# Four lanes of 24 to 28 quads instead of three of 32, with the later sorts' copies on GpSimd

## The chip, the cores and the metric

The kernel runs on one core of a Trainium2 chip. The metric is the device time of one execution in microseconds (us); lower is better. In the profile PE is TensorE's matmul, PEld its weight load, DVE VectorE, ACT ScalarE, POOL GpSimd and SP the engine that issues most of the DMAs.

## The reference

One layer of a graph network over V = 100,000 nodes of 64 channels and E = 3,300,000 edges, which come sorted by their target:

```python
h = jnp.maximum(_layernorm(x, axis=-1), 0.0)
local, nbr = h[dst], h[src]
y = jnp.concatenate([local, nbr - local], axis=-1) @ W.T + b      # per edge
s, cnt = segment_sum(y, dst, V), segment_sum(1, dst, V)
out = x + where(cnt > 0, s / max(cnt, 1), 0)
```

The sum over a node's edges is linear, so the kernel needs, per node, the sum of its neighbours' h, the count of its edges, and the node's own h times a weight matrix (the "own part").

## The kernel before

**First stage** (lines 207 to 315): per step of 3,584 nodes it loads `xt`, makes h by layer norm and relu, splits h into three bf16 parts and writes them as rows of `h3`, so that a sum of the three is as good as fp32. It clears the accumulator `acc` in DRAM, and it makes the own part (transpose on PE, copy `hT` on ACT, two matmuls, copy `own` on ACT) and writes that to `hb`.

**Two ways for the edges.** 384 windows of 8,064 consecutive edges go through a sort; what is left over, 57 chunks of 3,584 edges, is gathered. For a chunk (`chunks`, line 365) GpSimd issues 28 indirect DMAs of 128 rows of `h3` each (`nb`, line 403), DVE makes one-hot matrices `hot`, and PE sums the rows per target into `ps`.

**Lanes.** A lane is a set of windows, one per partition. `sort_lane` (line 430) loads a window's targets and sources, packs both into a key, and sorts the 8,192 keys of each partition by source with a merge network. `exchange` (line 468) is one step of it on a piece of at most 1,536 (lane 0) or 1,024 keys: a copy of the lower halves to `tmp` on ACT (line 469), then a min and a max on DVE (lines 470 and 471). Lane 0 has its `tmp` in PSUM, the later ones in SBUF. `fill_lane` (line 635) then fetches the sorted keys of each of the 157 source blocks of 640 nodes by indirect DMA (`kf`, line 650; `kx`, line 735) and writes tables of slots for the next stage (`sr_d`, `dt_d`).

**Quads.** `quads` (line 761) takes four windows at a time. For every source block it needs a one-hot `gh` (DVE, line 809) that picks rows of the block's table `tab` by matmul into `gp` (line 832), a cast of `gp` to `gs` on ACT (line 834), a second one-hot `dh` (DVE, line 360), and matmuls of both into `total` (line 841). Four blocks are a group: one `gh`, one `dh`, up to 24 matmuls of line 832 and 64 of line 841. `gh` has two buffers, `gp` two in lane 0 and three later. Tables of three blocks each are streamed from DRAM for each quad (727.5 KB a load), but every `STAY`th one is kept in SBUF (`stay`): none in lane 0, every 6th in lane 1, every 3rd in lane 2. A quad has 2,592 matmuls of line 841, so their count says how many quads a stretch holds.

**What runs beside what.** The sort of lane 0 runs with the chunks' gathers; `fill_lane(0)` follows. Then the quads of lane l run with the sort and the fill of lane l+1 between them: after each pick of a block (a `yield` of `quads`) `SORT` is taken from `spent`, and sort steps are issued until their estimates (`2.083 * n + 290` for n keys, close to ns) have filled it again. Lane 0's quads also carry the chunks that are left; the last lane runs alone, in a loop of two turns. After that come corrections for windows that share a node, and a last stage (line 1049) that divides, multiplies by the other weight matrix and writes `out`. The framework orders each engine's instructions by a schedule of its own, so a sort step can stand earlier than its place in the code.

Of the kernel before, what the change touches and what calls it, by code (L numbers as in the profile page):

```python
# [32 lines left out]
LANES = 3  # L33
# [5 lines left out]
STEP = 1000  # L39
SORT = 260  # L40
STAY = None, 6, 3
# [20 lines left out]
PIECES = 1536, 1024, 1024  # L62
# [23 lines left out]
def plan(v, e):  # L86

    wl = 1 << int(np.log2(33 * CH * 1.05))
    ew = wl - PAD
    nw = LANES * P  # L90
    return wl, nw, -(-(e - nw * ew) // CHUNK)
# [3 lines left out]
def gnn_preln(ctx: ExitStack, tc, x, src_w, dst_w, src_p, dst_p, src_a, dst_a, wT, b, out, V, E):  # L95
# [27 lines left out]
    SETS = NL * G  # L123
# [11 lines left out]
    assert 2 * C == P and SL % GP == 0 and NCB % GP and G % TURNS == 0  # L135
# [50 lines left out]

    x_v = x.rearrange("(p t) c -> p t c", p=P)
# [19 lines left out]
    with tc.tile_pool(name="pre", bufs=2) as pre, tc.tile_pool(name="small", bufs=4) as small, \  # L207
# [19 lines left out]
        b_sb = pre.tile([P, C], F32, name="b_sb", bufs=1)  # L227
        nc.sync.dma_start(b_sb, b.to_broadcast([P, C]))
        b3 = pre.tile([3 * 32, 2, C], BF16, name="b3", bufs=1)
        nc.vector.memset(b3, 0.0)  # L230
        b_part = pre.tile([P, C], BF16, name="b_part", bufs=1)
        for i in range(3):
            nc.vector.tensor_copy(b_part, b_sb)
            nc.vector.tensor_sub(b_sb, b_sb, b_part)
            nc.vector.tensor_copy(b3[32 * i:32 * i + 1], b_part[32 * i:32 * i + 1, None, :].to_broadcast([1, 2, C]))
        ones3 = pre.tile([3 * 32, P], BF16, name="ones3", bufs=1)
        nc.vector.memset(ones3, 1.0)


# [34 lines left out]
        for t in range(0, NPT, T):  # L274
            load_x(t + 2 * T)
            nc.sync.dma_start(acc_v[:, t:t + T], zeros)
            xt = xts.pop(t)
            st = st_ps.tile([P, 5, T], F32, name="st")
            nc.vector.tensor_reduce(st[:, 0], xt, axis=AX.X, op=ALU.add)
            nc.vector.tensor_scalar_mul(st[:, 1], st[:, 0], 1.0 / C)  # L280
            nc.vector.tensor_sub(xt, xt, st[:, 1, :, None].to_broadcast([P, T, C]))
            sq = pre.tile([P, T, C], F32, name="sq", bufs=3)
            nc.scalar.activation(sq, xt, AF.Square)
            nc.vector.tensor_reduce(st[:, 2], sq, axis=AX.X, op=ALU.add)
            nc.scalar.activation(st[:, 3], st[:, 2], AF.Sqrt, bias=eps, scale=1.0 / C)
            nc.vector.reciprocal(st[:, 4], st[:, 3])
            nc.vector.scalar_tensor_tensor(xt, xt, 0.0, st[:, 4, :, None].to_broadcast([P, T, C]), op0=ALU.max, op1=ALU.mult)

            parts = pre.tile([P, T, CT], BF16, name="parts", bufs=3)
            nc.gpsimd.memset(parts[:, :, C3:], 1.0)  # L290
            nc.scalar.copy(parts[:, :, :C], xt)
            nc.gpsimd.tensor_tensor(sq, xt, parts[:, :, :C], ALU.subtract)
            nc.scalar.copy(parts[:, :, C:2 * C], sq)
            nc.gpsimd.tensor_tensor(parts[:, :, 2 * C:C3], sq, parts[:, :, C:2 * C], ALU.subtract)
            nc.sync.dma_start(h3_v[:, t:t + T], parts)
            own = pre.tile([P, T, C], F32, name="own")
            for u in range(0, T, SUB):
                n = min(SUB, T - u)
                t_ps = st_ps.tile([P, SUB // 2, P], F32, name="t_ps")
                for i in range(n // 2):  # L300
                    nc.tensor.transpose(t_ps[:, i], xt[:, u + 2 * i:u + 2 * i + 2].rearrange("p a c -> p (a c)"), ident)
                hT = pre.tile([P, SUB // 2, P], F32, name="hT")
                nc.scalar.copy(hT[:, :n // 2], t_ps[:, :n // 2])  # L303
                o_ps = st_ps.tile([P, SUB, C], F32, name="o_ps")
                o2 = o_ps.rearrange("p (i a) c -> p i (a c)", a=2)
                for i in range(n // 2):
                    nc.tensor.matmul(o2[:, i], lhsT=ones3, rhs=b3.rearrange("p a c -> p (a c)"), start=True, stop=False)
                    nc.tensor.matmul(o2[:, i], lhsT=hT[:, i], rhs=w_own.rearrange("p a c -> p (a c)"),  # L308
                                     start=False, stop=True)
                nc.scalar.copy(own[:, u:u + n], o_ps[:, :n])  # L310
# [6 lines left out]
    with tc.tile_pool(name="few", bufs=1) as few, ExitStack() as early:  # L317
# [17 lines left out]
        def store(base, at, tiles):  # L335

            with after(SP):
                row = nc.values_load(base, engines=[SP], min_val=0, max_val=V)
                for i, part in enumerate(tiles):
                    if i:  # L340
                        nc.sync.dma_start(acc[ds(row + i * P, P)], part)
                    else:
                        last[SP] = nc.sync.dma_start(shared[at], part[0:1])
                        nc.sync.dma_start(acc[ds(row + 1, P - 1)], part[1:])

        later = []
# [5 lines left out]
        def add_now(all_of_them=False):  # L352
            while later and (all_of_them or (later[0][0] <= count[0] and count[0] - count[1] >= GAP)):
                later.pop(0)[1]()
                count[1] = count[0]
# [9 lines left out]
        def chunks(n):  # L365
# [22 lines left out]
            for k in range(n * parts + 1):  # L388
                q, part = divmod(k, parts)
                u = q % KG  # L390
                if q < n:
                    if u == 0 and part == 0:
                        si, near = ahead
                    hot = rows.tile([P, JH, P], BF16, name="hot", bufs=4)
# [21 lines left out]
                if before is not None and before[2] == parts - 1:  # L416
                    sums = rows.tile([P, C1], F32, name="sums", bufs=LAG + 2)
# [9 lines left out]
        def drain(events):  # L427
            for _ in events:
                pass
        def sort_lane(l, keys, piece, few, ps):  # L430
# [13 lines left out]
            mine = slice(l * P, l * P + P)  # L444
            for x in range(2):
                for i in range(W):
                    nc.sync.dma_start(wb_d[x, mine].rearrange("(g i) o -> i g o", i=W)[i], wb_i[i * G:i * G + G, x:x + 1])
                nc.sync.dma_start(wb_r[:, x, mine], wb_d[x, mine].rearrange("w o -> o w"))
# [19 lines left out]
            def exchange(lo, hi, tmp):  # L468
                last[ACT] = nc.scalar.copy(tmp, lo)  # L469
                nc.vector.tensor_tensor(lo, tmp, hi, ALU.min)  # L470
                last[DVE] = nc.vector.tensor_tensor(hi, tmp, hi, ALU.max)  # L471

            def merge(p, k):
# [3 lines left out]
                def blocks(b, q, m):  # L477
                    r = keys[:, 2 * p * b:2 * p * (b + q)].rearrange("p (b l) -> p b l", l=2 * p)
                    if k < p:
# [4 lines left out]
                             tmp[:, :q * m * k].rearrange("p (b m t) -> p b m t", b=q, t=k))  # L484

                def run(a, n):
                    tmp = ps.tile([P, PIECE], F32, name="tmp")
                    exchange(keys[:, a:a + n], keys[:, a + k:a + k + n], tmp[:, :n])

                def groups(a, n):  # L490
                    r = keys[:, a:a + 2 * k * n].rearrange("p (m s t) -> p m s t", s=2, t=k)
                    tmp = ps.tile([P, PIECE], F32, name="tmp")
                    exchange(r[:, :, 0], r[:, :, 1], tmp[:, :n * k].rearrange("p (m t) -> p m t", t=k))
# [72 lines left out]
            for t in range(len(tail) + 2 * regions):  # L566
                for i in range(regions):
                    q = t - 2 * i
                    if 0 <= q < len(tail):
# [8 lines left out]
                        if q == len(tail) - 1:  # L578
                            ready = min(span * (i + 1), WL)
# [5 lines left out]
            assert ready == WL  # L585
# [49 lines left out]
        def fill_lane(l, piece, took):  # L635
# [3 lines left out]
            mine = slice(l * G, l * G + G)  # L639
# [16 lines left out]
            def spread(numbers, n, to):  # L656
# [90 lines left out]
            nc.sync.dma_start(xs_d[:, mine], xg)  # L747
# [161 lines left out]

        def behind_quads(l, aside):  # L910
# [9 lines left out]
        with tc.tile_pool(name="keys", bufs=1) as big, tc.tile_pool(name="piece", bufs=2) as piece, \  # L920
                tc.tile_pool(name="sort_ps", bufs=2, space=PSUM) as ps:
            for i, ns in enumerate(sort_lane(0, big.tile([P, WL], F32, name="keys"), piece, few, ps)):
                k = i - 40
                if 0 <= k < NCB:
                    with tc.issue_after(last[ACT].ins):
                        nc.scalar.dma_start(tables[k // TG, :, k % TG].rearrange("p (b f) -> p b f", b=NB),
                                            h3[k * CS:(k + 1) * CS].rearrange("(b p) f -> p b f", b=NB))
                gathers(ns)

        for l in range(NL):  # L930
            with ExitStack() as aside:
# [7 lines left out]
                else:  # L939
                    early.close()  # L940
                with tc.tile_pool(name="load", bufs=3) as load, tc.tile_pool(name="hots", bufs=3) as hots, \
                        tc.tile_pool(name="g_ps", bufs=3 if l else 2, space=PSUM) as g_ps, \
# [3 lines left out]
                    if l == NL - 1:  # L946
                        with tc.For_i(0, TURNS, 1) as g:
                            drain(quads(l * G + g * (G // TURNS), G // TURNS, kept))
# [11 lines left out]
                    if l == 0:  # L960
                        drain(ev)
# [163 lines left out]
```

## Time and profile before

| What | us |
|---|---|
| median of 3 runs (lowest, highest) | 22121.42 (22117.3, 22134.35) |
| the profiled execution, whole | 22127.49 |
| its span, first to last instruction | 22125.9 |
| mean granted TensorE clock | 0.869 of full |

The profiled execution is 6.1 us above the median. Its span falls into stages, and the engines' busy shares over the whole span mix them, so the reading goes by stage: where each stage begins and ends is seen by which lines run in it. The first stage ends near 460 us, the sort of lane 0 near 1650, the first fill at 2013, lane 0's quads at 10000, lane 1's at 16560, lane 2's at 21770.

### The profile page before, as it was taken

To read this page: it belongs to the slowest core of one execution; us is meant where nothing else is said; L and a number is where in the kernel's file an instruction comes from. 1 tells how busy PE (TensorE), PEld (TensorE's weight loads), DVE (VectorE), ACT (ScalarE), POOL (GpSimd) and SP (SyncE) were. 2 spreads that over 40 slices of the span, in tenths; PEclk is the share of its full clock that TensorE was granted. 3 is DMA by queue.
4 is the path that set the end of the run, shared out by engine and by line. 5 is a ranking of instruction groups with operands and counts; after the bars stand their busy time and mean duration, and the time that the engine had idled before them with its cause. 6 is when DMAs were issued, how large, how long until landed. Compare 5 with 4: busy or idle time off the path is not lost. (4 is left out here: it accounts for less than half of the span.)

```text
span 22125.9 us, 770402 instructions
## 1 busy us (share of the span) xinstructions
PE 16188.9 (73%) x343607; PEld 13895.5 (63%) x343607; DVE 15051.3 (68%) x13757; ACT 8886.6 (40%) x17494; POOL 2886.3 (13%) x2647
## 2 busy tenths in 40 slices
PE   5102556567777688887777777776888999899996
PEld 4002444456665577776666666665777888788886
DVE  8894444457665566667777777765767777777775
ACT  4342222234443344443444444533444444444442
POOL 5763333310002100000000000011000000000003
PEclk7556777788888899999999999987999999999998
DMA  6544545566666677786666666666777777677777
GB/s 247 80 68 114 160 150 159 154 194 223 214 226 217 212 266 267 268 268 225 217 219 214 217 218 212 218 209 181 260 257 239 241 235 238 227 231 241 236 239 261
DMA packets 1821829, 4713.39 MB, mean 213 GB/s; under 512 B 951238, under 2 KB 959697, under 8 KB 1813057
## 3 DMA queue, kind: packets, MB, share of 16 engines
q1 hardware_dynamic: 1629646, 4493.73, 61.7%
q0 software_dynamic: 80656, 105.27, 3.0%
q10 hardware_dynamic: 108188, 64.99, 1.4%
q8 instruction: 2692, 44.11, 0.8%
q14 instruction: 647, 5.30, 0.1%
HBM read 4466.78 MB, written 235.40 MB: 213 GB/s over the span
## 5 line engine op out<-in xcount | busy, mean ns | idle before, releaser
L832 PEld LDWEIGHTS <-gh 128*128 128x128 bf16 x90432 | 7799.2, 101 | 4935.9 <-issue 3557.5
L834 ACT CAST gs<-gp 128x386 bf16<-128x386 f32 x15072 | 7131.9, 482 | 9211.9 <-PE gp L832 8091.3
L832 PE MATMUL gp<-tab,gh 128*128 128x193 bf16 x75264 | 7998.1, 258 | 3657.2 <-ACT gs L834 1727.4
L809 DVE TENSOR_TENSOR gh<-srs,c 128x3072 bf16<-128x3072 int16 (+1 forms) x3840 | 6617.0, 1723 | 4745.8 <-PE gp L832 4452.1
L841 PE MATMUL total<-gs,dh 32*128 32x193 bf16 x241152 | 6720.4, 255 | 591.8 <-issue 567.0
L841 PEld LDWEIGHTS <-dh 32*128 32x128 bf16 x241152 | 5408.2, 98 | 1656.2 <-issue 1612.1
L360 DVE TENSOR_TENSOR dh<-dt,c 128x2048 bf16<-128x2048 int16 (+1 forms) x3840 | 4586.7, 1194 | 1499.2 <-PE total L841 775.2
L469 ACT COPY tmp<-keys 128x1024 f32<-128x1024 f32 (+16 forms) x948 | 1017.0, 1081 | 2727.5 <-DVE keys L471 2380.5
L798 POOL DMA_INDIRECT rows_x<-h,xs x192 | 181.9, 947 | 14093.4 <-PE total L841 10876.8
L403 POOL DMA_INDIRECT nb<-h,si x1596 | 1633.0, 1023 | 2097.8 <-PE ps L408 1573.2
L832 PE MATMUL gp<-stay,gh 128*128 128x193 bf16 x15168 | 1536.4, 250 | 161.3 <-ACT gs L834 147.9
L471 DVE TENSOR_TENSOR keys<-tmp,keys 128x1024 f32<-128x1024 f32 (+16 forms) x948 | 1173.6, 1252 | 19.8
L470 DVE TENSOR_TENSOR keys<-tmp,keys 128x1024 f32<-128x1024 f32 (+14 forms) x948 | 1160.7, 1239 | 17.1 <-ACT tmp L469 16.3
L408 PE MATMUL ps<-nb,hot 128*128 128x193 bf16 x1596 | 357.9, 307 | 1059.8 <-DVE sums L421 673.6
L408 PEld LDWEIGHTS <-hot 128*128 128x128 bf16 x1596 | 190.0, 122 | 1098.1 <-DVE sums L421 682.1
L650 POOL DMA_INDIRECT kf<-ksort,at_i x483 | 459.9, 952 | 1073.3 <-ACT k L691 908.9
L860 DVE SCALAR_TENSOR_TENSOR whole<-own,whole 128x193 f32<-128x193 bf16 x768 | 285.7, 414 | 123.4 <-ACT whole L856 123.3
L856 ACT COPY whole<-total 128x388 f32<-128x388 f32 x384 | 157.4, 497 | 237.9 <-PE total L841 218.1
L864 DVE TENSOR_REDUCE wsums<-whole 128x128 f32<-128x384 f32 x384 | 226.9, 591 | 0.1
L308 PEld LDWEIGHTS o_ps<-w_own,hT 128*128 128x128 f32 x784 | 160.7, 260 | 94.9 <-ACT hT L303 84.3
L735 POOL DMA_INDIRECT kx<-ksort,xat x192 | 181.1, 943 | 298.0 <-DVE xat L732 240.4
L308 PE MATMUL o_ps<-w_own,hT 128*128 128x128 f32 x784 | 193.5, 386 | 14.8 <-ACT hT L303 14.2
(189 smaller groups left out, 3677.7 us busy)
## 6 DMA issues: line engine op xcount, KB each, us to landing
tab<-tables SPq DMA_DIRECT2D x4160, 727.5 KB
srs<-sr_d SPq DMA_DIRECT2D x1824, 512.0 KB
tables<-h ACTq DMA_DIRECT2D x157, 242.5 KB
h<-parts SPq DMA_DIRECT2D x28, 1358.0 KB
own<-h SPq DMA_DIRECT2D x384, 97.0 KB
srs<-sr_d SPq DMA_DIRECT2D x96, 320.0 KB
dt_d<-t SPq DMA_DIRECT2D x57, 512.0 KB
dt<-dt_d SPq DMA_DIRECT2D x1824, 16.0 KB
```

What stands on the lines that cost most here:

```text
L308: nc.tensor.matmul(o2[:, i], lhsT=hT[:, i], rhs=w_own.rearrange("p a c -> p (a c)"), start=False, stop=True)
L360: nc.vector.tensor_tensor(out.rearrange("p k (a d) -> p k a d", d=D), numbers[:, :, None].to_broadcast(shape), upto[:shape[0], :n].rearran ...
L403: last[POOL] = nc.gpsimd.indirect_dma_start(out=nb[:, j], out_offset=None, in_=h3, in_offset=bass.IndirectOffsetOnAxis(ap=si[:, u, at:at + ...
L408: nc.tensor.matmul(ps, lhsT=before[0][:, j], rhs=before[1][:, j, :CE], start=before[2] == 0 and j == 0, stop=before[2] == parts - 1 and j ...
L469: last[ACT] = nc.scalar.copy(tmp, lo)
L470: nc.vector.tensor_tensor(lo, tmp, hi, ALU.min)
L471: last[DVE] = nc.vector.tensor_tensor(hi, tmp, hi, ALU.max)
L650: last[POOL] = nc.gpsimd.indirect_dma_start(out=kf[:, c], out_offset=None, in_=ksort, in_offset=bass.IndirectOffsetOnAxis(ap=at_i[:, c0 + ...
L809: last["hots"] = nc.vector.tensor_tensor(gh[:, :m].rearrange("p c i b s -> p (c i) b s"), srs[u, s // SL][:, c:c + m].rearrange("p c i s - ...
L832: nc.tensor.matmul(gp[:, i], lhsT=ghots[u, s][:, i, b], rhs=row[:, b + i * (NB - NR), :CE], start=b == 0, stop=b == NR - 1)
L834: nc.scalar.copy(gs[u, s], gp)
L841: nc.tensor.matmul(total[:, i, to(b)], lhsT=hot[at, b * P:b * P + P], rhs=of[at], start=flags.get("start", False) and b == 0, stop=flags.g ...
```

## The change

The number of lanes goes from three of 32 quads to four of 24, 24, 24 and 28, so 400 windows are sorted instead of 384, and 21 chunks are gathered instead of 57. All chunks are issued before the first quads (`drain(ev)` stands ahead of them), so lane 0's quads no longer share PSUM and SBUF with them: they get three `gp` buffers and every 6th table kept; `STAY` is 6, 6, 6, 3. Each lane still sorts 128 partitions; those without a window of their own repeat another. The fill writes only the rows of the lane's own quads. `SORT` goes from 260 to 340. Lane 0's pieces shrink from 1,536 to 1,024 keys. In lanes 1 to 3 the copy to `tmp` moves from ACT to GpSimd and is issued one piece ahead: the min and max of the piece before follow it (`held`). The own part leaves the first stage: that writes h itself to `hb`, and `own_part` reads it back, makes the product and writes it again, one step per sort step of lane 0 from the tenth on; the clearing of `acc` goes there too, on ACT's queue instead of SP's.

```diff
+QUADS = 24, 24, 24, 28
+LANES = len(QUADS)
-STEP = 1000
-SORT = 260
-STAY = None, 6, 3
+SORT = 340
+STAY = 6, 6, 6, 3
-PIECES = 1536, 1024, 1024
+PIECES = 1024, 1024, 1024, 1024
+HEAD = 10
...
         for t in range(0, NPT, T):
-            nc.sync.dma_start(acc_v[:, t:t + T], zeros)
...
-            own = pre.tile([P, T, C], F32, name="own")
-            for u in range(0, T, SUB):
...
-            nc.scalar.dma_start(hb_v[:, t:t + T], own)
+            nc.scalar.dma_start(hb_v[:, t:t + T], xt)
...
-            def exchange(lo, hi, tmp):
-                last[ACT] = nc.scalar.copy(tmp, lo)
-                nc.vector.tensor_tensor(lo, tmp, hi, ALU.min)
-                last[DVE] = nc.vector.tensor_tensor(hi, tmp, hi, ALU.max)
+            def compare():
+                if held:
+                    lo, hi, tmp, _ = held.pop()
+                    nc.vector.tensor_tensor(lo, tmp, hi, ALU.min)
+                    last[DVE] = nc.vector.tensor_tensor(hi, tmp, hi, ALU.max)
+
+            def exchange(lo, hi, tmp, *of):
+                if l == 0:
+                    last[ACT] = nc.scalar.copy(tmp, lo)
+                    held.append((lo, hi, tmp, of))
+                    return compare()
+                if held and any(a < y and x < z for a, z in of for x, y in held[0][3]):
+                    compare()
+                nc.gpsimd.tensor_copy(tmp, lo)
+                compare()
+                held.append((lo, hi, tmp, of))
...
-                nc.sync.dma_start(to.rearrange("p g (c d) -> p g c d", d=D), t4[:, :, :n])
+                nc.sync.dma_start(to.rearrange("p g (c d) -> p g c d", d=D), t4[:, :ng, :n])
...
                 for i in range(W):
                     nc.sync.dma_start(sr_d[mine, c0:c0 + m, :, i * KS:i * KS + KS],
-                                      s16[i * G:i * G + G].rearrange("g c (h s) -> g c h s", h=2))
+                                      s16[i * G:i * G + ng].rearrange("g c (h s) -> g c h s", h=2))
...
+        def own_part(pool, own_ps):
+            zeros = pool.tile([P, T, C1], F32, name="zeros", bufs=1)
+            nc.gpsimd.memset(zeros, 0.0)
+            yield
+            for t in range(0, NPT, T):
+                nc.scalar.dma_start(acc_v[:, t:t + T], zeros)
+                yield
+            cleared.append(True)
+            for t in range(0, NPT, T):
+                ht = pool.tile([P, T, C], F32, name="ht")
+                nc.sync.dma_start(ht, hb_v[:, t:t + T])
+                own = pool.tile([P, T, C], F32, name="own")
+                for u in range(0, T, SUB):
...
+                    nc.scalar.copy(hT[:, :n // 2], t_ps[:, :n // 2])
+                    yield
...
+                    nc.scalar.copy(own[:, u:u + n], o_ps[:, :n])
+                    yield
+                nc.sync.dma_start(hb_v[:, t:t + T], own)
...
+                if i >= HEAD:
+                    next(owns, None)
                 gathers(ns)
+            drain(owns)
...
-                else:
+                    drain(ev)
                     early.close()
...
-                        tc.tile_pool(name="g_ps", bufs=3 if l else 2, space=PSUM) as g_ps, \
+                        tc.tile_pool(name="g_ps", bufs=3, space=PSUM) as g_ps, \
...
-                    for _ in quads(l * G, G, kept):
-                        if l == 0:
-                            gathers(STEP)
+                    for _ in quads(BASES[l], QUADS[l], kept):
                         spent -= SORT
```

How the work lies on the engines now is shown at three places.

ACT, in the quads of lane 1 before, while lane 2's sort runs behind them (`gs<-gp` is the cast that frees a `gp` buffer for PE, `tmp<-keys` the sort's copy):

```order
L834 CAST gs<-gp 128x386 x4
L469 COPY tmp<-keys 128x1020
L834 CAST gs<-gp 128x386 x12
L469 COPY tmp<-keys 128x780
L834 CAST gs<-gp 128x386 x8
L469 COPY tmp<-keys 128x992
```

ACT, in the quads of lane 0 of the changed kernel, with lane 1's sort behind them (`whole<-total` reads a finished quad):

```order
L841 CAST gs<-gp 128x386 x157
L863 COPY whole<-total 128x388 x4
L841 CAST gs<-gp 128x386 x20
L552 ACTIVATE junk,pos<-keys,bound 128x258 x4
L841 CAST gs<-gp 128x386
L552 ACTIVATE junk,pos<-keys,bound 128x258
```

A sort copy stood after every 4, 8 or 12 casts; now whole quads of 157 casts pass without one, and only the counts at the sort's end (`junk`) stand between casts.

DVE, late in a sort behind quads, before:

```order
L809 TENSOR_TENSOR gh_218070<-srs_217848,c32_107 128x3072
L470 TENSOR_TENSOR keys_155545<-tmp_218083,keys_155545 128x31x32
L471 TENSOR_TENSOR keys_155545<-tmp_218083,keys_155545 128x31x32
L360 TENSOR_TENSOR dh_218072<-dt_217850,c32_107 128x2048
L809 TENSOR_TENSOR gh_218180<-srs_218064,c32_107 128x3072
L360 TENSOR_TENSOR dh_218182<-dt_218066,c32_107 128x2048
L809 TENSOR_TENSOR gh_218292<-srs_218064,c32_107 128x3072
L470 TENSOR_TENSOR keys_155545<-tmp_218314,keys_155545 128x31x32
```

DVE at such a place of the changed kernel:

```order
L347 TENSOR_TENSOR dh_174205<-dt_173979,c32_123 128x2048
L816 TENSOR_TENSOR gh_174315<-srs_174197,c32_123 128x3072
L461 TENSOR_TENSOR keys_116822<-tmp_174216,keys_116822 128x31x32
L462 TENSOR_TENSOR keys_116822<-tmp_174216,keys_116822 128x31x32
L347 TENSOR_TENSOR dh_174317<-dt_174199,c32_123 128x2048
L816 TENSOR_TENSOR gh_174429<-srs_174197,c32_123 128x3072
L347 TENSOR_TENSOR dh_174431<-dt_174199,c32_123 128x2048
L816 TENSOR_TENSOR gh_174533<-srs_174423,c32_123 128x3072
L461 TENSOR_TENSOR keys_116822<-tmp_174355,keys_116822 128x32x32
```

The pattern is the same, one or two groups per pair of compares; by the code a pair comes every 1.8 groups instead of every 2.3. The numbers behind the names count up in the order of the code: the pair in the first fence works on a `tmp` (218083) newer than the `gh` ahead of it (218070), the pair in the second on one (174216) older than its `gh` (174315), a piece behind.

POOL, from the sort of lane 0 to the first quads, before (`nb` are the chunks' gathers, `kf` and `kx` the fill's):

```order
L625 IOTA row 128x1 x3
L403 DMA nb<-h_61,si 128x194 x770
L643 IOTA first 128x157
L650 DMA kf<-ksort,at_i 128x64 x161
L735 DMA kx<-ksort,xat 128x1 x64
```

POOL at the start of the same stretch of the changed kernel:

```order
L390 DMA nb<-h_61,si 128x194 x70
L471 COPY tmp<-keys 128x1024 x8
L650 IOTA first 128x157
L471 COPY tmp<-keys 128x1024
L657 DMA kf<-ksort,at_i 128x64 x43
L471 COPY tmp<-keys 128x1024
L657 DMA kf<-ksort,at_i 128x64 x3
```

All 588 gathers of the chunks stand ahead of the fill now, and lane 1's copies stand between the fill's gathers, where POOL had gathers alone.

More of the change, by code (lines that the diff above doesn't have):

```diff
@@ L89, in plan @@
     ew = wl - PAD
-    nw = LANES * P
+    nw = sum(QUADS) * W
     return wl, nw, -(-(e - nw * ew) // CHUNK)
@@ L122, in gnn_preln @@
     WL = EW + PAD
-    SETS = NL * G
+    BASES = [sum(QUADS[:l]) for l in range(NL)]
+    SETS = sum(QUADS)
     NCB = -(-V // CS)
@@ L134, in gnn_preln @@
     assert NT == 2 and NB == 5 and W * KS == P and 2 * CE + NT <= 512
-    assert 2 * C == P and SL % GP == 0 and NCB % GP and G % TURNS == 0
+    assert 2 * C == P and SL % GP == 0 and NCB % GP and QUADS[-1] % TURNS == 0 and max(QUADS) <= G
     consts = ctx.enter_context(tc.tile_pool(name="consts", bufs=1))
@@ L185, in gnn_preln @@
     nc.vector.memset(odd, 0.0)
+    b_sb = consts.tile([P, C], F32, name="b_sb")
+    nc.sync.dma_start(b_sb, b.to_broadcast([P, C]))
+    b3 = consts.tile([3 * 32, 2, C], BF16, name="b3")
+    nc.vector.memset(b3, 0.0)
+    b_part = consts.tile([P, C], BF16, name="b_part")
+    for i in range(3):
+        nc.vector.tensor_copy(b_part, b_sb)
+        nc.vector.tensor_sub(b_sb, b_sb, b_part)
+        nc.vector.tensor_copy(b3[32 * i:32 * i + 1], b_part[32 * i:32 * i + 1, None, :].to_broadcast([1, 2, C]))
+    ones3 = consts.tile([3 * 32, P], BF16, name="ones3")
+    nc.vector.memset(ones3, 1.0)
     x_v = x.rearrange("(p t) c -> p t c", p=P)
@@ L335, in store @@
         def store(base, at, tiles):
+            assert cleared
             with after(SP):
@@ L352, in add_now @@
         def add_now(all_of_them=False):
-            while later and (all_of_them or (later[0][0] <= count[0] and count[0] - count[1] >= GAP)):
+            while later and cleared and (all_of_them or (later[0][0] <= count[0] and count[0] - count[1] >= GAP)):
                 later.pop(0)[1]()
@@ L578, in sort_lane @@
                         if q == len(tail) - 1:
+                            compare()
                             ready = min(span * (i + 1), WL)
@@ L584, in sort_lane @@
                                     keys[:, a:ready].bitcast(I32))
-            assert ready == WL
+            assert ready == WL and not held
             if l == NL - 1:
@@ L908, in took @@
             owed -= GATHER
+        def own_part(pool, own_ps):
[11 more added lines that the diff above has]
+                for u in range(0, T, SUB):
+                    n = min(SUB, T - u)
+                    t_ps = own_ps.tile([P, SUB // 2, P], F32, name="t_ps")
+                    for i in range(n // 2):
+                        nc.tensor.transpose(t_ps[:, i], ht[:, u + 2 * i:u + 2 * i + 2].rearrange("p a c -> p (a c)"), ident)
+                    hT = pool.tile([P, SUB // 2, P], F32, name="hT")
+                    nc.scalar.copy(hT[:, :n // 2], t_ps[:, :n // 2])
+                    yield
+                    o_ps = own_ps.tile([P, SUB, C], F32, name="o_ps")
+                    o2 = o_ps.rearrange("p (i a) c -> p i (a c)", a=2)
+                    for i in range(n // 2):
+                        nc.tensor.matmul(o2[:, i], lhsT=ones3, rhs=b3.rearrange("p a c -> p (a c)"), start=True, stop=False)
+                        nc.tensor.matmul(o2[:, i], lhsT=hT[:, i], rhs=w_own.rearrange("p a c -> p (a c)"),
+                                         start=False, stop=True)
+                    nc.scalar.copy(own[:, u:u + n], o_ps[:, :n])
+                    yield
+                nc.sync.dma_start(hb_v[:, t:t + T], own)
         def behind_quads(l, aside):
@@ L920, in gnn_preln @@
         with tc.tile_pool(name="keys", bufs=1) as big, tc.tile_pool(name="piece", bufs=2) as piece, \
-                tc.tile_pool(name="sort_ps", bufs=2, space=PSUM) as ps:
+                tc.tile_pool(name="sort_ps", bufs=2, space=PSUM) as ps, \
+                tc.tile_pool(name="own", bufs=2) as own, tc.tile_pool(name="own_ps", bufs=1, space=PSUM) as own_ps:
+            owns = own_part(own, own_ps)
             for i, ns in enumerate(sort_lane(0, big.tile([P, WL], F32, name="keys"), piece, few, ps)):
@@ L947, in gnn_preln @@
                         with tc.For_i(0, TURNS, 1) as g:
-                            drain(quads(l * G + g * (G // TURNS), G // TURNS, kept))
+                            drain(quads(BASES[l] + g * (QUADS[l] // TURNS), QUADS[l] // TURNS, kept))
                             add_now(True)
@@ L1102, in by_lane @@
     def by_lane(a):
-        return np.ascontiguousarray(a.reshape(LANES, G, W, ew).transpose(0, 2, 1, 3)).reshape(LANES, P, ew)
+        lanes = np.split(a.reshape(sum(QUADS), W, ew), np.cumsum(QUADS)[:-1])
+        lanes = [np.concatenate([q, np.repeat(q[-1:], G - len(q), axis=0)]) for q in lanes]
+        return np.ascontiguousarray(np.stack(lanes).transpose(0, 2, 1, 3)).reshape(LANES, P, ew)
     nf = -(-E // (P * JA))
```

52 lines of the change are left out of this document (16 added, 36 removed).

## The prediction

> **What bounds the kernel now.** I read the first page for the span, then the busy times cut into stages, since the shares over the whole span mix stages with different limits. Columns: the stretch, its length, then busy us and number of instructions of PE, PEld, DVE, ACT and POOL, the granted clock, the DMA engines' share and GB/s.
>
> ```profile
> span 22125.9 us, 770402 instructions
> PE 16188.9 (73%) x343607; PEld 13895.5 (63%) x343607; DVE 15051.3 (68%) x13757; ACT 8886.6 (40%) x17494; POOL 2886.3 (13%) x2647
> ...
> 0.00:460.00 460.00, 272.87 (x1570) 231.10 (x1570) 373.36 (x279) 256.69 (x346) 215.40 (x111) 0.77 0.72 275
> 460.00:1650.00 1190.00, 119.86 (x700) 92.24 (x700) 1072.64 (x1033) 472.17 (x520) 841.03 (x774) 0.52 0.48 77
> 1650.00:2013.00 363.00, 0.00 (x0) 0.00 (x0) 132.30 (x394) 50.85 (x42) 214.51 (x223) 0.50 0.30 51
> 2013.00:10000.00 7987.00, 5832.46 (x113819) 4765.45 (x113819) 4657.91 (x4280) 2774.30 (x5610) 1072.77 (x1126) 0.84 0.67 213
> 10000.00:10045.00 45.00, 12.55 (x345) 11.43 (x342) 23.31 (x22) 5.97 (x13) 1.36 (x1) 0.64 0.44 163
> 10045.00:14450.00 4405.00, 3376.14 (x76074) 2973.07 (x76078) 3429.53 (x2931) 1969.07 (x3982) 39.76 (x42) 0.93 0.67 218
> 15500.00:16500.00 1000.00, 883.64 (x20847) 783.51 (x20846) 707.46 (x575) 452.44 (x950) 9.45 (x10) 0.97 0.79 260
> 16605.00:21770.00 5165.00, 4709.36 (x113088) 4199.27 (x113088) 3837.24 (x3104) 2458.08 (x5152) 62.02 (x65) 0.98 0.72 235
> 21770.00:22126.00 356.00, 200.81 (x1177) 182.00 (x1177) 142.77 (x250) 56.08 (x112) 208.55 (x61) 0.77 0.77 292
> ```
>
> The same cut for line 841 alone counts quads, at 2,592 matmuls each:
>
> ```profile
> 2013.00:10000.00 7987.00, 2621.94 (x82784) 2002.82 (x82784) 0.84 0.67 213
> ...
> 10045.00:14450.00 4405.00, 1440.20 (x55764) 1218.10 (x55768) 0.93 0.67 218
> 14500.00:15400.00 900.00, 274.32 (x8618) 203.88 (x8617) 0.78 0.61 182
> 15500.00:16500.00 1000.00, 379.82 (x15296) 317.21 (x15296) 0.97 0.79 260
> 16605.00:21770.00 5165.00, 2034.78 (x82944) 1695.36 (x82944) 0.98 0.72 235
> ```
>
> So a quad takes 250 us in lane 0 (7987 for 31.94), 204.8 in lane 1 with a sort behind it (4405 for 21.51), 270.7 with a fill (900 for 3.325), 169.5 alone with every 6th table kept (1000 for 5.90) and 161.4 alone with every 3rd (5165 for 32.0). Alone, PE leads with 88 and 91% busy. Behind a sort neither leads: PE 77%, DVE 78%, so I asked what they wait for there (line, what it waited for: us, times, longest):
>
> ```profile
> ACT tmp L469 <- DVE keys L471: 1191.8, 328, 8.7
> ACT gs L834 <- PE gp L832: 1157.8, 730, 16.8
> ...
> DVE gh L809 <- PE gp L832: 857.2, 726, 8.1
> PE gp L832 <- ACT gs L834: 810.5, 326, 5.5
> ```
>
> And in order of time, one piece of it (start, duration, in brackets the idle time before and what ended it):
>
> ```profile
> 12004.42 1.16 DVE L471 TENSOR_TENSOR keys<-tmp,keys 128x960 f32<-128x960 f32 x1
> ...
> 12005.61 1.02 ACT L469 COPY tmp<-keys 128x992 f32<-128x992 f32 x1 [3.51 <-DVE keys L471]
> ...
> 12006.53 1.77 ACT L834 CAST gs<-gp 128x386 bf16<-128x386 f32 x4
> 12007.06 0.67 PE L832 MATMUL gp<-tab,gh 128*128 128x193 bf16 x6 [2.45 <-ACT gs L834]
> ...
> 12007.76 1.75 DVE L809 TENSOR_TENSOR gh<-srs,c 128x3072 bf16<-128x3072 int16 x1 [1.06 <-PE gp L832]
> ...
> 12011.35 1.75 DVE L809 TENSOR_TENSOR gh<-srs,c 128x3072 bf16<-128x3072 int16 x1 [0.71 <-PE gp L832]
> ...
> 12017.62 1.75 DVE L809 TENSOR_TENSOR gh<-srs,c 128x3072 bf16<-128x3072 int16 x1 [1.06 <-PE gp L832]
> ```
>
> This is the reading that decides. ACT's queue is in order: the next piece's copy stands there, waits 3.51 us until DVE's max of the piece before is done (12005.58), and the casts behind it wait with it. PE has no free `gp`, stands 2.45 us, and its lateness keeps `gh`'s buffer, so DVE waits 1.06 us. A group with a compare pair takes 6.27 us (12011.35 to 12017.62), one without 3.59. PE stood for ACT 326 times, once for nearly each piece of the sort.
>
> **The change, part by part.**
>
> *The copies leave ACT (lanes 1 to 3).* The 810.5 us in which PE waited for casts lose their cause: no sort copy stands between casts, and a copy issued a piece ahead has some two groups, over 5 us, to finish. What is late next is DVE. Its work per quad is 3837.24 / 32 = 119.9 us in the lane that runs alone and 3429.53 / 21.51 = 159.4 behind the sort, so a sort is (159.4 - 119.9) x 21.51 = 850 us of DVE. With `SORT` at 340 it fills 21.51 x 260/340 = 16.45 quads, and DVE has 119.9 + 850/16.45 = 171.6 us a quad. That is the lower bound. With DVE as little busy as before (78%) it would be 220. The engine that leads alone reaches 88 and 91%; nearest to that, and a touch better since DVE needs no table, I take 92%: 186 us a quad.
>
> *The price of a copy on POOL* stands in no row. Its nearest rows are a write of 1,820 words and a two-input operation on 1,792:
>
> ```profile
> L1071 POOL TENSOR_TENSOR ht<-ht,xo 128x1792 f32<-128x1792 f32 x28 | 111.3, 3976 | 2.2
> L220 POOL MEMSET zeros<- 128x1820 f32 x1 | 1.6, 1607 | 0.0
> L469 ACT COPY tmp<-keys 128x1024 f32<-128x1024 f32 x278 | 296.7, 1069 | 899.5 <-DVE keys L471 833.8 <-issue 50.6 <-DVE keys L463 11.0
> L470 DVE TENSOR_TENSOR keys<-tmp,keys 128x1024 f32<-128x1024 f32 x278 | 342.0, 1232 | 4.9 <-ACT tmp L469 4.9
> L470 DVE TENSOR_TENSOR keys<-tmp,keys 128x1536 f32<-128x1536 f32 x93 | 163.2, 1767 | 1.1 <-ACT tmp L469 0.7 <-issue 0.4
> ```
>
> That bounds 1,024 keys between 0.90 us and 2.27 us; ACT takes 1.07. Behind quads any of these hides under two groups. If that cover went, 927 copies (below) would cost 0.8 to 2.1 ms. DVE's one-hots are not slowed where GpSimd works beside them, with gathers (first row, 2500 to 4500 us) or with next to none (second, 17000 to 20000 us):
>
> ```profile
> L809 DVE TENSOR_TENSOR gh<-srs,c 128x3072 bf16<-128x3072 int16 x218 | 375.1, 1721 | 331.5 <-PE gp L832 306.2 <-issue 14.4 <-remote 8.8
> L809 DVE TENSOR_TENSOR gh<-srs,c 128x3072 bf16<-128x3072 int16 (+1 forms) x744 | 1281.8, 1723 | 676.2 <-PE gp L832 640.9 <-DMA dt<-dt_d 30.3 <-DMA srs<-sr_d 4.5
> ```
>
> The Trainium skill (SBUF — State Buffer, Who interferes with whom) speaks against the change: a DVE instruction with two SBUF inputs and a GpSimd instruction that reads SBUF exclude each other for a whole instruction. By that rule the compares, whose `tmp` now lies in SBUF beside `keys`, can meet a copy; the one-hots, with one input in PSUM, cannot. No run here shows it yet. A copy is free to start when the pair before it ends and the next pair comes groups later, so I expect them to pass each other, and by the rule the sum stays; what it would be otherwise is the second rival.
>
> *One more lane.* Its sort and its fill come on top, but part of lane 1's sort runs before any quads, and did before as well. Of 339 pairs to a lane (first row, lane 2's sort) 249 lay in lane 0's quads (second), so 90 were done with the sort of lane 0 (third):
>
> ```profile
> 10045.00:16605.00 6560.00, 394.54 (x339) 0.91 0.68 221
> ...
> 2013.00:10000.00 7987.00, 291.20 (x249) 0.84 0.67 213
> ...
> 460.00:1650.00 1190.00, 465.58 (x353) 0.52 0.48 77
> ```
>
> The schedule should keep that, so 249/339 x 16.45 = 12.1 quads run behind a sort in lane 0 and 16.45 in lanes 1 and 2: 45.0 quads, with 249 + 339 + 339 = 927 copies on POOL. The other 72 - 45 = 27.0 run alone or with a fill. The sum: 45.0 x 186 = 8,370 (7,720 by the lower bound, 9,216 at lane 1's pace of before, 9,900 at 220); 27.0 x 169.5 = 4,577.
>
> *Fills, changes of lane, last lane.* A fill cost 900 - 3.325 x 169.5 = 336 us beyond its quads. Its writes now cover 24 of 32 rows: between 252 and 336; most of its work is not writes, so 300, three times: 900. A change of lane loads the kept tables, 45 us, twice: 90. The last lane has `STAY` 3 as before: 45 + 28 x 161.4 = 4,564. The stage after the quads stays at 356.
>
> *Chunks.* Gathers of line 403 before the quads and in lane 0's quads:
>
> ```profile
> 0.00:2013.00 2013.00, 838.83 (x770) 0.58 0.50 118
> 2013.00:10000.00 7987.00, 794.19 (x826) 0.84 0.67 213
> ```
>
> The 826 go, and with them what took lane 0 from 204.8 (with a sort, no chunks) to 250 a quad. That is in the pace already taken for lane 0, for which the kept tables and the third `gp` speak too. Now 588 run, all before the quads: no more than there were, so I cost them at nothing.
>
> *Before the quads* (2013 us). DVE is busy 373.4 + 1072.6 = 1,446 of the first 1,650 us and idle 204. Of that some 215 go (the schedule shows lane 1's copies between the fill's gathers, so 90 pairs at 2 x 1.2 us move into the fill). Lane 0's smaller pieces add 34: 2.41 ns a key (2 x 1232/1024) for 2.30 (2 x 1767/1536), over some 328,000 keys. So DVE has 1,265, and with 165 of the idle time left (it shrinks with the pairs) the fill could begin at 1,430. The own part comes between: 224 copies like this one,
>
> ```profile
> L310 ACT COPY own<-o_ps 128x512 f32<-128x512 f32 x84 | 47.9, 588 | 27.5 <-PE o_ps L308 27.4
> ```
>
> at most 132 us of ACT, busy 472 of 1,190 there. Each stands ahead of the sort's copies, waiting for PE, which waits for the chunks' one-hots; 28 loads, 28 writes and the clearing's 28 writes are queued with the chunks' loads. If all hides, it costs nothing; if each copy stops the sort for 1.3 us, about as long as a compare, 290. I take 60, since the gathers and ACT have slack: 1,490. The fill took 363 with POOL busy 214.5; 90 copies at 0.90 to 2.27 add 81 to 204, in part in its idle time: 455. Loading the kept tables (9 loads of 727.5 KB) at the 260 GB/s of quads alone is 25. Quads at 1,970, between 1,850 and 2,150. The first stage also loses own part and clearing (28 x 910 KB of its 127 MB); it waits on DVE and DMA in turn, so that is in the lower end.
>
> **The sum**: 1,970 + 8,370 + 4,577 + 900 + 90 + 4,564 + 356 = 20,827. The execution had 1.6 us outside its span (22127.49 against 22125.9) and stood 6.1 above the median, so set against the median it is some 20,825; call it 20,830, 5.8% faster.
>
> **The rivals.**
> 1. *Slower: each copy shuts DVE out.* As a mechanism here: DVE always has an instruction with SBUF operands in hand, and POOL's copy stops it for its whole length. 927 x 0.90 to 2.27 = 830 to 2,100 us: 21,660 to 22,930. It ends slower from (22,127 - 20,829) / 927 = 1.40 us a copy. Against it stand the `gh` rows above, though a gather reads little; the compares are a fifth of DVE's time. Chance 0.07. This is the rule of the Trainium skill told above, at its worst.
> 2. *The sort costs what it did.* Behind quads it added 4405 - 21.51 x 169.5 = 759 us. If the quads wait for DVE's compares rather than for ACT's copies, the denser sort loses as much each: 45.0/16.45 x 759 = 2,076 against 45.0 x (186 - 169.5) = 743 in the sum, so 22,160, no gain. For it: DVE's queue is in order too, and each pair delays the next `gh` by 2.4 us. Against: PE stood 810 us for ACT alone. Chance 0.06.
> 3. *Half of it.* DVE waits for late copies or tables and reaches 82 to 88% (195 to 209 us a quad: +400 to +1,035), or the own part holds up the first sort. 21,200 to 21,900; chance 0.12.
> 4. *Better.* DVE runs full behind sorts: 45.0 x (186 - 171.6) = 650 less, 20,180, and the fills and the start may come in lower. 20,000 to 20,500; chance 0.15.
>
> **How the numbers follow.** My forecast, 20,500 to 21,200, has 0.60. The range leaves out the upper half of what is slower and little below: 20,200 to 21,650 holds 8 in 10. A measurement of this kernel tells about 0.2% (44 us) from no change. Slower by more: rivals 1 above 1.40 us, and 2 with a late start, 0.08; within it 0.03; faster 0.89.
>
> **What the profile after would show.** Right: no PE wait for the cast (`gp` <- ACT `gs`) of any size behind a sort; DVE over 90% busy there and PE waiting for DVE's `gh`; POOL's copy at about 1 to 1.5 us with the compares' mean still 1.23 and `gh`'s 1.72; matmuls of the cast's pick in lane 0 at the pace of lanes 1 and 2; first quad near 1,970. Wrong: DVE waiting for POOL's `tmp`, or `gh` and compares lengthened beside a copy (rival 1); DVE and PE both under 85% behind a sort (2 and 3); a fill that begins after 1,600.

## The result, and the profile after

The changed kernel takes 21478.42 us (median of 4 runs, 21464.65 to 21506.48) where the kernel before takes 22127.88 (4 runs, 22117.3 to 22151.66): a ratio of 0.9707, 95% interval 0.969 to 0.9723. It is 2.9% faster: inside the wide range (20,200 to 21,650), outside the forecast of 20,500 to 21,200, and half of the 5.8% that was forecast. The profiled execution has a span of 21477.2, 650 us more than the sum of 20,827.

The first page for the changed kernel, span and busy times:

```profile
span 21477.2 us, 800717 instructions
PE 16114.3 (75%) x356735; PEld 14138.2 (66%) x356735; DVE 16347.9 (76%) x15424; ACT 8776.8 (41%) x17753; POOL 3157.3 (15%) x2899
```

The stretches of the start, all engines (columns as in the prediction: PE, PEld, DVE, ACT, POOL, then clock, DMA share, GB/s). The first fill's gathers begin at 1757 (before: 1648), the first quad at 2327 (before: 2013):

```profile
0.00:350.00 350.00, 1.01 (x3) 0.26 (x3) 275.36 (x211) 147.09 (x114) 206.79 (x107) 1.00 0.79 304
350.00:1757.00 1407.00, 401.10 (x2155) 329.12 (x2155) 980.95 (x1045) 505.75 (x737) 593.26 (x604) 0.60 0.58 110
1757.00:2327.00 570.00, 0.00 (x0) 0.00 (x0) 335.44 (x566) 50.88 (x42) 359.28 (x308) 0.50 0.16 30
```

Lane 2 cut by what runs behind its quads, the matmuls into `total` alone (line 848 now, 2,592 to a quad; columns PE, PEld): the sort's loading, its compares, its counts on ACT, its counts on DVE, the fill, and quads alone.

```profile
11794.00:12047.00 253.00, 79.98 (x3104) 67.42 (x3104) 0.91 0.71 230
12047.00:14642.00 2595.00, 910.16 (x36096) 763.37 (x36096) 0.93 0.72 238
14642.00:14805.00 163.00, 52.38 (x1728) 44.26 (x1728) 0.86 0.59 197
14805.00:14974.00 169.00, 58.58 (x2376) 49.45 (x2380) 0.94 0.75 250
14974.00:15945.00 971.00, 299.54 (x9700) 228.81 (x9688) 0.80 0.62 187
15945.00:16535.00 590.00, 225.58 (x9216) 189.12 (x9216) 0.97 0.79 261
```

Behind the compares a quad takes 2595 / (36096/2592) = 186.3 us, the 186 of the forecast. The same stretch for all engines, and what its engines waited for:

```profile
12047.00:14642.00 2595.00, 2156.96 (x49212) 1897.52 (x49212) 2361.67 (x2001) 1070.94 (x2241) 358.37 (x351) 0.93 0.72 238
```

```profile
POOL tmp L471 <- DVE keys L462: 2225.6, 316, 38.1
ACT gs L841 <- PE gp L839: 1459.3, 799, 8.0
PE gp L839 <- DMA tab<-tables: 345.5, 148, 6.1
DVE gh L816 <- PE gp L839: 201.0, 106, 8.1
...
PE gp L839 <- DVE gh L816: 51.6, 37, 5.2
...
PE gp L839 <- ACT gs L841: 1.8, 3, 0.6
```

DVE is busy 2361.67 of 2595, 91%. PE's wait for the cast, 810.5 us behind the sort of before, is 1.8 us. No wait of DVE for POOL's `tmp` is in the list; POOL waits for DVE. PE's largest wait is now for tables (345.5 us), not for DVE's `gh` (51.6), which the prediction had named as the sign. The instructions themselves, in the same stretch:

```profile
L816 DVE TENSOR_TENSOR gh<-srs,c 128x3072 bf16<-128x3072 int16 x543 | 949.2, 1748 | 205.8 <-PE gp L839 201.0 <-DMA srs<-sr_d 4.1
...
L461 DVE TENSOR_TENSOR keys<-tmp,keys 128x1024 f32<-128x1024 f32 x121 | 148.9, 1231 | 0.0
L471 POOL COPY tmp<-keys 128x1024 f32<-128x1024 f32 x120 | 128.2, 1069 | 888.7 <-DVE keys L462 878.6 <-DVE keys L461 10.1
```

A copy of 1,024 keys takes 1069 ns on POOL, as long as it took on ACT. The compare keeps its 1.23 us and `gh` takes 1748 ns instead of 1721. The rule of the Trainium skill (SBUF — State Buffer, Who interferes with whom), by which a DVE instruction with two SBUF inputs and a GpSimd instruction that reads SBUF exclude each other, costs nothing that these rows show. They hardly put it to the test: most copies start only when a pair has ended, as POOL's 2225.6 us of waiting for DVE say, and the next pair comes groups later.

### The profile page after: what moved, and what is told of

The parts are those of the page before. It is cut to its first block, busy times and chain, and to the rows that moved or that the text cites. A ratio compares the mean times of both kernels' runs of the same rounds, so it can differ in the third digit from the quotient of the medians.

```text
span 21477.2 us, 800717 instructions
## 1 busy us (share of the span) xinstructions
PE 16114.3 (75%) x356735; PEld 14138.2 (66%) x356735; DVE 16347.9 (76%) x15424; ACT 8776.8 (41%) x17753; POOL 3157.3 (15%) x2899
## 5 line engine op out<-in xcount | busy, mean ns | idle before, releaser
L841 ACT CAST gs<-gp 128x386 bf16<-128x386 f32 x15700 | 7525.0, 483 | 10278.3 <-PE gp L839 9566.2
L839 PEld LDWEIGHTS <-gh 128*128 128x128 bf16 x94200 | 8125.3, 101 | 4504.5 <-issue 2309.0
L839 PE MATMUL gp<-tab,gh 128*128 128x193 bf16 x73800 | 7573.3, 257 | 3461.7 <-DMA tab<-tables 1847.8
L816 DVE TENSOR_TENSOR gh<-srs,c 128x3072 bf16<-128x3072 int16 (+1 forms) x4000 | 6883.8, 1721 | 3257.3 <-PE gp L839 2953.3
L839 PE MATMUL gp<-stay,gh 128*128 128x193 bf16 x20400 | 2078.6, 251 | 49.9 <-ACT gs L841 36.6
L471 POOL COPY tmp<-keys 128x1024 f32<-128x1024 f32 (+13 forms) x1017 | 1057.7, 1041 | 7133.7 <-DVE keys L462 6618.4
L461 DVE TENSOR_TENSOR keys<-tmp,keys 128x1024 f32<-128x1024 f32 (+10 forms) x1356 | 1599.6, 1184 | 500.3 <-ACT tmp L466 238.4
L462 DVE TENSOR_TENSOR keys<-tmp,keys 128x1024 f32<-128x1024 f32 (+10 forms) x1356 | 1578.1, 1170 | 35.6
L657 POOL DMA_INDIRECT kf<-ksort,at_i x644 | 659.2, 1024 | 1502.1 <-ACT k L698 1318.6
L390 POOL DMA_INDIRECT nb<-h,si x588 | 579.6, 986 | 537.7 <-PE ps L395 277.6
L466 ACT COPY tmp<-keys 128x1024 f32<-128x1024 f32 (+9 forms) x339 | 337.8, 1003 | 403.7 <-DVE keys L462 168.7
L395 PE MATMUL ps<-nb,hot 128*128 128x193 bf16 x588 | 88.7, 322 | 320.4 <-DVE sums L408 252.9
```

What stands on the lines that cost most here:

```text
L390: last[POOL] = nc.gpsimd.indirect_dma_start(out=nb[:, j], out_offset=None, in_=h3, in_offset=bass.IndirectOffsetOnAxis(ap=si[:, u, at:at + ...
L471: nc.gpsimd.tensor_copy(tmp, lo)
L657: last[POOL] = nc.gpsimd.indirect_dma_start(out=kf[:, c], out_offset=None, in_=ksort, in_offset=bass.IndirectOffsetOnAxis(ap=at_i[:, c0 + ...
L816: last["hots"] = nc.vector.tensor_tensor(gh[:, :m].rearrange("p c i b s -> p (c i) b s"), srs[u, s // SL][:, c:c + m].rearrange("p c i s - ...
L839: nc.tensor.matmul(gp[:, i], lhsT=ghots[u, s][:, i, b], rhs=row[:, b + i * (NB - NR), :CE], start=b == 0, stop=b == NR - 1)
L841: nc.scalar.copy(gs[u, s], gp)
```

## Experiments

The eight ran on two other chips of the same kind. On the second chip (later copies back on ACT, copies on POOL alone, own part back, tables' writes on SP) the kernel before takes 20,907 us, on the third (the other four) 20,898, not 22,128. Ratios are to it, so they are compared among themselves and not with 0.9707; where a run of the second chip is set beside one of the third, only the near-equal time of the kernel before speaks for it.

Two readings of the late first quad are told apart. Theory A: the own part's copies and DMA issues on ACT hold up lane 0's sort. Theory B: lane 1's early copies do, which stand on POOL behind the chunks' gathers.

**The changed kernel and the kernel before on the third chip**, with no edit.

> The changed kernel itself, on the same chip as the runs beside it. The first experiments ran on a chip on which the kernel before took 20,907 us instead of 22,128, so their ratios have no partner. If the change is worth the same share everywhere, the ratio is 0.969 to 0.972 again. If the gain hung on how slowly gathers and quads go side by side on the first chip (351 us a quad with chunks, 260 with a fill), it is smaller where that costs less: 0.98 to 0.995.

Measured: 20,644.69 us, ratio 0.988 (0.9863 to 0.9896). The gain is 1.2% there, by the second expectation: it hangs on the chip.

> The kernel before, for its trace on this chip. If chips differ in what gathers cost beside quads, lane 1's fill takes about 205 to 215 us a quad instead of 260 and lane 0 with chunks 230 to 300 instead of 351, while the pace alone (169.5, 161.4) and behind a sort (about 203) stays as it was. If a chip is slower throughout, all paces differ alike.

Measured: one run, 20,919.56. The matmuls into `total` (PE, PEld), first in lane 0 with chunks on the first chip, then on the third, then on the third behind lane 2's sort:

```profile
2800.00:3600.00 800.00, 196.80 (x5568) 145.93 (x5568) 0.73 0.51 154
```

```profile
2800.00:3600.00 800.00, 234.78 (x8448) 196.72 (x8436) 0.89 0.73 234
...
9400.00:13400.00 4000.00, 1316.49 (x50284) 1113.43 (x50272) 0.93 0.65 215
```

A quad with chunks takes 372 us on the first chip and 245 on the third; behind a sort alone 206.2, near the first chip's 204.8. With lane 1's fill it takes 282 on the first (849 us for 7,812 matmuls) and 226 on the third (726 for 8,332), more than the 205 to 215 expected. So in the kernel before the chips differ most where GpSimd issues many indirect DMAs beside quads.

**Later copies back on ACT**, and no longer a piece ahead.

```diff
-                if l == 0:
-                    last[ACT] = nc.scalar.copy(tmp, lo)
-                    held.append((lo, hi, tmp, of))
-                    return compare()
-                ...
-                nc.gpsimd.tensor_copy(tmp, lo)
-                compare()
-                held.append((lo, hi, tmp, of))
+                last[ACT] = nc.scalar.copy(tmp, lo)
+                held.append((lo, hi, tmp, of))
+                return compare()
```

> The changed kernel with the later lanes' copies back on ACT and no longer a piece ahead, SORT still 340. If the copies on POOL are what lets DVE run at 92% behind a sort (186 us a quad), the pace goes to 200 to 215 and 46 such quads cost 650 to 1,300 us: 22,100 to 22,800. If the pace comes from the kept tables, the third gp buffer and the chunks' leaving, it stays below 190 and the time within 150: 21,330 to 21,630. By theory B the first quad comes 100 to 200 us earlier than 2,327; by A it does not.

Measured: 21,800.6, ratio 1.0431 (1.0414 to 1.0449): by the ratios some 1,150 us slower than the changed kernel, 4.3% slower than before. Its waits in 2,000 us behind lane 2's sort, and the stretch:

```profile
ACT tmp L465 <- DVE keys L462: 757.8, 211, 8.5
...
PE gp L833 <- ACT gs L835: 485.2, 203, 5.5
```

```profile
12600.00:14600.00 2000.00, 1473.53 (x32712) 1292.86 (x32705) 1590.66 (x1328) 867.15 (x1705) 17.48 (x18) 0.93 0.62 205
```

PE's wait for casts is back and DVE falls to 80% busy. By matmuls (23,976 in this stretch) a quad takes 216 us; in the changed kernel on the third chip 11700 to 13700 holds 27,864, 186 a quad. The kept tables and the third `gp` buffer, which this kernel has too, did not give the pace. The run undoes the engine and the order together; copies on ACT a piece ahead were not tried. Its first quad comes at 1,985, against 2,104 in the changed kernel: the copies that help behind quads cost time ahead of them.

**Copies on POOL alone, in the kernel before.** The edit puts `held`, `compare` and the changed `exchange` into the kernel before; three lanes, `SORT` 260 and chunks as they were.

> The kernel before with one part of the change alone: the later lanes' copies on POOL and a piece ahead; three lanes, SORT 260 and the chunks as before. If the cast's queue was the stall, lane 1's 204.8 us a quad behind the sort falls to 175 to 182 and it gains 500 to 640 there, and 200 to 500 in lane 0, which has the chunks: 21,000 to 21,450. If the copies help only together with a denser sort, or if the chunks' gathers on POOL delay them, 21,700 to 22,100.

Measured: 20,339.52, ratio 0.9729 (0.9711 to 0.9747): 567 us faster, though its first quad comes at 2,322 instead of 1,958. Behind lane 2's sort a quad takes 178.7 us (9200 to 12500: 47,872 matmuls) instead of 206.2, inside the 175 to 182 expected, with DVE 88% busy. `SORT`, the kept tables and the `gp` buffers of that lane are as they were, so the copies alone give this pace. As a ratio the expected time was 0.949 to 0.969; the late first quad is what it misses that by. Its waits before the first quad:

```profile
DVE keys L473 <- POOL tmp L483: 371.8, 30, 84.6
```

Lane 1's first pairs stand in DVE's queue, their copies stand in POOL's queue behind the chunks' gathers, and lane 0's sort waits behind them on DVE. In the longest of these waits, 84.6 us that end at 635, POOL issues one `nb` gather after another, and then the copy.

**Early copies on ACT.** Copies issued before the first quads go to ACT, in the changed kernel and in the kernel before with its copies on POOL:

```diff
+        begun = []
...
-                if l == 0:
+                if l == 0 or not begun:
                     last[ACT] = nc.scalar.copy(tmp, lo)
...
                             if k % 3 == 0:
                                 next(rest)
+                        begun.append(True)
```

> The changed kernel with the copies of lane 1's first sort steps, those issued before the first quads, on ACT as before; all later copies stay on POOL. Theory B, those copies stand on POOL behind the chunks' gathers and DVE's queue waits for them: the first quad comes at 1,950 to 2,050 instead of 2,150 to 2,330 and the time falls by 150 to 350 us against the changed kernel. Theory A, the own part on ACT is what delays the sort: no change or up to 60 us slower.

Measured: 20,535.93, ratio 0.983 (0.9812 to 0.9848), 109 us less than the changed kernel: less than the 150 to 350 expected, though the first quad comes at 1,970 as expected. The sort's and the fill's stretches, first in the changed kernel on the third chip, then here:

```profile
350.00:1536.00 1186.00, 409.23 (x2155) 337.75 (x2155) 979.98 (x1044) 505.28 (x737) 591.82 (x604) 0.61 0.64 131
1536.00:2104.00 568.00, 0.00 (x0) 0.00 (x0) 334.39 (x567) 50.87 (x42) 358.62 (x307) 0.50 0.14 30
```

```profile
350.00:1521.00 1171.00, 386.02 (x2155) 317.85 (x2155) 983.62 (x1049) 518.90 (x749) 573.85 (x595) 0.63 0.64 132
1521.00:1970.00 449.00, 0.00 (x0) 0.00 (x0) 285.81 (x563) 128.33 (x120) 279.04 (x227) 0.50 0.18 38
```

With the copies on POOL the fill's gathers stand behind copies that wait for DVE, and the fill takes 119 us more; lane 0's sort before it takes nearly the same (1,186 and 1,171).

> The kernel before with the copies on POOL a piece ahead, except those before the first quads, which stay on ACT: three lanes. By theory B the first quad comes near 2,000 instead of 2,300, 0.955 to 0.963 of the time before. If the lateness has another cause there, 0.971 to 0.975 as in the run with all copies on POOL. If this lies below the changed kernel, the fourth lane, the own part's move and SORT 340 together cost time.

Measured: 19,968.71, ratio 0.9557 (0.9538 to 0.9576), first quad at 1,962: as theory B has it. It beats the changed kernel in the same comparison by 676 us. Three lanes are ahead there: what else the change has (fourth lane and fewer chunks, `SORT` 340, moved own part, lane 0's smaller pieces and kept tables) together costs 567 us when both have their early copies on ACT (20,536 against 19,969). Which part costs it was not tried apart with the early copies on ACT. Behind lane 2's sort its matmuls into `total` give 177.6 us a quad:

```profile
9100.00:11900.00 2800.00, 1015.63 (x40860) 853.00 (x40864) 0.94 0.73 248
```

**Own part back in the first stage, and the tables' writes on SP.**

```diff
             load_x(t + 2 * T)
+            nc.sync.dma_start(acc_v[:, t:t + T], zeros)
...
-            nc.scalar.dma_start(hb_v[:, t:t + T], xt)
+            own = pre.tile([P, T, C], F32, name="own")
+            ...
+            nc.scalar.dma_start(hb_v[:, t:t + T], own)
...
-            owns = own_part(own, own_ps)
+            owns = iter(())
```

> The changed kernel with one part undone: the own part and the clearing of acc go back into the first stage. Theory A, the own part's copies and DMA issues on ACT hold up lane 0's sort: the first stage ends near 460 us again, the sort takes 1,190 less the 180 us of DVE work that left it, the fill 574, so the first quad comes near 2,050 instead of 2,327 and the time is 21,190 to 21,260. Rival B, the late start comes from lane 1's copies, which now stand behind the gathers on POOL and so run in the fill: the sort keeps its idle time, the first stage gets 110 us longer, 21,480 to 21,590.

```diff
-                        nc.scalar.dma_start(tables[k // TG, ...
+                        nc.sync.dma_start(tables[k // TG, ...
```

> The changed kernel with the 157 writes of the tables (tables<-h) issued by SP instead of ACT, nothing else. ACT spent 333 us on these issues in lane 0's sort, against some 120 before. If it is this that holds up the sort's copies (theory A2), the fill begins 100 to 200 us earlier: 21,280 to 21,380. If it is the own part's copies, which wait on ACT for PE (theory A1), or POOL's order (B), nothing moves: 21,440 to 21,510.

Measured: 20,713.94 (0.9906, 0.989 to 0.9923) and 20,709.5 (0.9901, 0.9885 to 0.9918), against the changed kernel's 0.988: no gain from either, by intervals that just overlap with its own. The expected times were set for the first chip; read as ratios to the changed kernel, theory A had 0.987 to 0.990 for the own part and rival B 1.000 to 1.005, and 1.003 came. With the tables' writes on SP (on ACT they take 333 us in the changed kernel, 93 in the kernel before) the fill begins at 1,607, not earlier than 1,536. With the own part back, it begins at 1,845, and DVE's wait for POOL stands in the sort:

```profile
DVE keys L477 <- POOL tmp L487: 271.9, 13, 85.3
```

So where lane 1's early copies do harm depends on the schedule: in the sort here and in the kernel before with POOL's copies, in the fill in the changed kernel.

## Why the prediction was right in part, and which steps failed

Against the profiled execution on the first chip, term by term (the rows of the lanes hold their fills):

| Step | Forecast | Measured |
|---|---|---|
| first quad | 1,970 | 2,327 |
| lane 0, 24 quads (2327 to 6962) | 4,568 | 4,635 |
| lane 1 (7000 to 11755) | 4,640 | 4,755 |
| lane 2 (11794 to 16535) | 4,640 | 4,741 |
| three changes of lane | 135 | 127 |
| lane 3, 28 quads | 4,519 | 4,522 |
| stage after the quads | 356 | 370 |

- *The copies leave ACT*: right, in mechanism and in size (186.3 for 186, DVE 91% for 92%, a share that was chosen and not derived). The kernel before with its copies on POOL alone shows that it is the copies, by engine and order together, that do it. Rivals 1 and 2 fell with it. (The `tmp` of the later lanes lay in SBUF in the kernel before as well; new is that GpSimd does the copy.)
- *Before the quads* is the step that failed: 357 of the 650 us missing, 90 in the fill and 267 ahead of it. It is in part rival 3's second condition, "the own part holds up the first sort" (21,200 to 21,900, chance 0.12), and the sign "a fill that begins after 1,600" came.
- The fill: I gave it 455 and the kept tables 25, and they took 570. I found the 90 early pairs and priced their copies at "81 to 204, in part in its idle time", as time on POOL only; the gathers queue behind copies that wait for DVE. On the third chip the run with early copies on ACT takes 119 us out of this fill. That its first quad comes at 1,970, the very number, is a coincidence of another kernel on another chip. I had asked for no wait on POOL in the order, though I quoted the copies between the fill's gathers.
- Ahead of the fill (begun at 1,757 instead of 1,490) DVE's work was right: 275.36 + 980.95 = 1,256 us for 1,265. Its idle time was not: 501 us, where I had 165 and the 60 of the own part. DVE's waits from 350 us to the first quad, in the changed kernel on the first chip, in the kernel before there, in the changed kernel on the third chip, and (500 to 1845) with the own part back on the second:

```profile
DVE keys L461 <- ACT tmp L466: 238.4, 83, 27.4
...
DVE keys L461 <- issue: 127.0, 26, 57.6
```

```profile
DVE keys L470 <- ACT tmp L469: 16.3, 8, 8.8
```

```profile
DVE keys L461 <- ACT tmp L466: 159.4, 105, 5.2
```

```profile
DVE keys L477 <- ACT tmp L482: 4.7, 9, 1.1
```

  So the 60 us for the own part was too small: with it between lane 0's copies on ACT, DVE waits 142 to 238 us for them in every run, and at most 34.9 in the runs where it is not there. Undoing it gained nothing on the second chip, since the wait for POOL's `tmp` (271.9) took its place; on the first chip it was not tried. The third chip begins the same fill at 1,536, 46 us behind the forecast, so 221 of the 267 us are the first chip's with this kernel (the kernel before: 1,648 and 1,582, 66 apart). The list of the third chip has no "issue" wait of these compares, which here is 127.0 us with no cause that the profile shows; why the first chip has it stays open.
- *Fills*: a fill has 971 us and 9,700 matmuls, 3.74 quads, so 971 - 3.74 x 169.5 = 337 us beyond its quads, where I took 300. Writing 24 of 32 rows made it no shorter. The fill's stretch of lane 1 in the kernel before:

```profile
14496.00:15474.00 978.00, 302.39 (x9664) 227.18 (x9664) 0.79 0.62 188
```

  By the code each of its steps is spread over two picks (`yield 2 * SORT`), whatever it writes; the equal counts agree. Three fills make +111. More than half of what a fill costs beyond its quads is the first chip's: to the end of its `kx` gathers it is 844 - 3.04 x 169.5 = 329 us there (14974 to 15818: 7,876 matmuls), and 720 - 3.38 x 169.5 = 147 on the third (14345 to 15065: 8,768).
- *Sort*: I spread 16.45 quads at 186. The compares have 13.9; the loading (253 us for 1.20 quads, 211 each) and the counts on ACT (163 us for 0.67, 245 each) are slower than that. This, with the fill, is what lanes 1 and 2 took too much.
- *Chunks*: their leaving was costed into lane 0's pace, and that held: lane 0 keeps 185 us a quad behind the sort (2400 to 4100: 23,840 matmuls). What I did not see is that the gain hangs on this chip's 372 us a quad with chunks, and is 1.2% where that is 245.

On the third chip the fourth lane seems not to pay. With three lanes and early copies on ACT, lane 0 with its chunks takes about 208 us a quad (6,640 for 32) and lane 1 about 183, so the chunks cost some 800 us there; against that stand four more quads (100 for 96, some 650 us), a sort's and a fill's excess. That is worked out from the stretches and not shown by a run of its own.

## What to carry to other kernels

Moving work off a queue that others wait on is worth what the waits behind it were: here 20 to 30 us a quad, near what was read from one wait in order of time. The same move must be followed to where the new queue has a backlog: a copy that stands behind gathers holds up not only its own queue but also the in-order engine that waits for it (371.8 us in the kernel before with its copies on POOL). Part of the move can be left out there: on the third chip the kernel before with only its later copies on POOL beat every other kernel tried there.

## What was not expected of the hardware

Chips of one kind run the same program 5.5% apart (22,128 us before on the first, 20,907 and 20,898 on the other two), and much of the difference lies beside indirect DMAs. In the changed kernel's last fill, while POOL issues the 64 `kx` gathers, PE almost stops on the first chip, one matmul into `total` about every 2.8 us with nothing in the profile that it waits for:

```profile
15772.49 0.94 POOL L742 DMA_INDIRECT kx<-ksort,xat  x1 [0.30 <-issue]
...
15774.67 0.32 PE L848 MATMUL total<-gs,dh 32*128 32x193 bf16 x1 [2.48 <-issue]
...
15777.47 0.32 PE L848 MATMUL total<-gs,dh 32*128 32x193 bf16 x1 [2.48 <-issue]
```

Matmuls into `total` in 80 us of these gathers, on the first chip and on the third:

```profile
15732.00:15812.00 80.00, 9.46 (x84) 3.41 (x72) 0.54 0.12 36
```

```profile
14980.00:15060.00 80.00, 25.48 (x928) 20.42 (x928) 0.86 0.46 164
```

84 against 928. Why the first chip does this is open.
